# A two-layer decoder on one core: layer 0's attentions in a line of their own, one pair at a time

## The chip, the core and the metric

The kernel runs on one NeuronCore of a Trainium2 chip, in fp32 throughout. The metric is the device time of one execution in microseconds (us), lower is better. TensorE (PE) multiplies, VectorE (DVE), ScalarE (ACT) and GpSimd (POOL) do the rest, and SyncE (SP) issues all DMAs in one queue.

## The reference, cut to what matters

32 batches of 56 tokens with 128 features pass two decoder layers; each step is added to its input and normalized (post-norm).

```python
x = ln(x + self_attn(x))                      # layer 0: 16 heads of 8, window of 32 tokens
x = ln(x + cross_attn(q=x, k=ctx, v=ctx))     # one head, ctx is 32 x 1500 x 128
x = ln(x + moe_gelu(x))                       # 8 experts of 512 units, top 2
x = ln(x + recurrence(x))                     # layer 1: conv over 3 tokens, gated scan, gate
x = ln(x + tanh(g) * cross_attn16(x, ctx))    # 16 heads of 64 over the same 1500 rows
x = ln(x + moe_swiglu(x))                     # shared expert and 8 experts of 256, top 2
```

In both mixtures every expert is computed for every token, and the router's weight (zero outside the top 2) multiplies its output. Layer 1's cross-attention is the large piece: its key and value projections are folded into the queries and the output, so that per batch 16 x 56 = 896 query columns meet 1500 context rows directly.

## The kernel before, in words

Two batches make a pair (112 tokens, TP), and there are 16 pairs. Layer 0 and layer 1's recurrence work on groups (`GROUPS`): pair 0 alone, pair 1 alone, then two pairs at a time, seven times.

The program is written by a planner in Python. Each stage is a generator which emits some instructions and then yields a latency in us, the time that it wants to pass before its next step. A `Thread` wraps it and adds up the PE time that it has spent, by the kernel's own table of costs. The order in which the threads are stepped gives the order in which instructions are emitted; the framework's scheduler makes every engine's queue from it, and stays near to it. PE executes its queue in order, so an instruction whose input is late holds everything behind it.

- `attention()` is the main thread, layer 1's cross-attention. Each batch is two blocks of 512 and 384 query columns. A block has 12 score products (`s<-qo,amT`, each copied by ACT at L1007), their maximum (DVE L1010, L1018), a shift (L1092), an exponential (ACT L1095), and 12 value products per 128 columns (`v<-amN,s`). Scores of one block stand beside values of the block before.
- `pre(g)` is everything ahead of it for group g: `self_attention`, `cross_attention_0`, `experts_0`, `recurrent_mixer`, `queries_1`. One thread per group; the threads run one after the other. `since` and `part` give the share of `PRE_US` that is due at this point of the main thread.
- `post(k)` is everything behind it for pairs 2k and 2k+1: the output projection (`f<-qo,n`) and `experts_1`. The last two pairs take `experts_1` one by one.
- `opening()` takes pairs 0 and 1 before the main thread starts, the second of them in borrowed memory (`place["aside"]`).
- When the main thread comes to a pair whose group is not ready, `finish` steps that thread to its end with nothing of the main thread between.

All products of `pre` and `post` go through two PSUM banks (pool `p_f`, tag f); scores have three (s), values two (v), transposes one (t).

Names that matter below. `normalize` and `normalize_twice` are a chain: sum (DVE), `moments` (two DVE instructions), two POOL instructions (L353, L354), a scaling on DVE (L356); their results `y`, `h`, `py` are then transposed on PE (L156). In `self_attention`, scores go through DVE (L436, L443), POOL (L444) and ACT (L448) before PE transposes them (`f<-ident,big`). `top2` is some 20 small DVE instructions behind the router; `wmix` is its result. `experts_0` uses the Gelu table of ACT (L684), while Exp and Tanh are in another. `experts_1` loads gate, up and down weights of each routed expert (three DMAs of 128 KB, tile `w`), with three buffers:

```python
t = wst.tile([P, 3 * U1], F32, tag="w1", name="w1", bufs=3)
```

Its loop issues the load of expert e, then gate and up products of the expert before it, then the down product (`f<-w,h`) of the one before that. `load_x0` brings the context for `cross_attention_0` (`cxN`), which also writes the transposed context to DRAM (`memT`) for the main thread's `amT`.

Of the kernel before, what the change touches and what calls it, by code (L numbers as in the profile page):

```python
# [15 lines left out]
TP = 2 * S  # L16
# [47 lines left out]
PRE_US, POST_US, PAIR_US = 74.0, 31.0, 80.5  # L64
# [5 lines left out]
def decoder_kernel(  # L70
# [33 lines left out]
    place = {"aside": None}  # L104

    def bank(pool, tag):
        if pool is p_f and place["aside"]:
            pool, tag = p_s, "s"
        return pool.tile([P, 512], F32, tag=tag, name=tag)
# [34 lines left out]
    clock = {"pe": 0.0}  # L144

# [44 lines left out]
    qpad0 = const.tile([P, G, 64], F32, name="qpad")  # L190
# [118 lines left out]
    def wide_tile(tag, n=T, bufs=1):  # L309
        return work.tile([P, T], F32, tag=tag, name=tag, bufs=bufs)[:, :n]  # L310
# [27 lines left out]
    def to_features(tiles, tag):  # L338
        t = wide_tile(tag)[:, : len(tiles) * TP]
        nc.vector.tensor_copy(t, transposed(tiles))  # L340
        return t
# [31 lines left out]
    def ahead(a, b, tag="res", bufs=2):  # L373
        r = tok_tile(tag, bufs)
        nc.gpsimd.tensor_tensor(r, a, b, ALU.add)  # L375
        return r
# [9 lines left out]
    HOP, NORM, LOAD = 2.5, 6.0, 14.0  # L386


    def self_attention(xs):
        nj, nt = len(xs), len(xs) * TP  # L390
        xT = to_features(xs, "xT")
        res = [ahead(t, obias) for t in xs]
        yield HOP
        qT, kT, oT = wide_tile("qT0", nt), wide_tile("kT0", nt), wide_tile("oT0", nt)
        affine(qT, linear(sqw("wq0"), xT, nt), vcol("bq0"))
        yield 0
        affine(kT, linear(sqw("wk0"), xT, nt), vcol("bk0"))
        yield 0
        vs, kbs = [], []
        for j in range(nj):  # L400

            v = hidden_tile().rearrange("p u t -> p (u t)")[:TP, : H0 * 32]
            v = v.rearrange("p (h f) -> p h f", h=H0)
            nc.vector.tensor_tensor(
                v.rearrange("p (i r) f -> p i r f", i=4),
                linear(pair(xT, j), sqw("wv0"), D, TP)
                .rearrange("p (i f) -> p i f", i=4).unsqueeze(2).to_broadcast([TP, 4, 4, 32]),
                vmask[:TP].unsqueeze(1).to_broadcast([TP, 4, 4, 32]),
                ALU.mult,
            )  # L410
            kb = mid.tile([P, 4, TP], F32, tag="kb", name="kb", bufs=2)
            nc.gpsimd.tensor_tensor(
                kb,
                pair(kT, j).unsqueeze(1).to_broadcast([P, 4, TP]),
                hmask4.unsqueeze(2).to_broadcast([P, 4, TP]),
                ALU.mult,
            )
            vs.append(v)
            kbs.append(kb)
            yield HOP  # L420
        w = 4 * TP
        for j in range(nj):
            s = big_tile(0)[:TP]
            s3 = s.rearrange("p (h k) -> p h k", h=H0)
            mx = tiny.tile([TP, H0], F32, tag="mx16", name="mx16")
            for i0 in (0, 2):
                pss = []
                for i in (i0, i0 + 1):

                    r = slice(32 * i, 32 * i + 32)  # L430
                    ps = bank(p_f, "f")
                    mm(ps[:TP, :w], pair(qT, j)[r], kbs[j][r].rearrange("p h k -> p (h k)"))
                    pss.append(ps)
                for i, ps in zip((i0, i0 + 1), pss):
                    c = slice(4 * i, 4 * i + 4)
                    nc.vector.scalar_tensor_tensor(  # L436
                        s3[:, c, :],
                        ps[:TP, :w].rearrange("p (h k) -> p h k", h=4),
                        DH0**-0.5,
                        wmask.unsqueeze(1).to_broadcast([TP, 4, TP]),  # L440
                        ALU.mult, ALU.add,
                    )
                    nc.vector.tensor_reduce(mx[:, c], s3[:, c, :], AX.X, ALU.max)  # L443
                    nc.gpsimd.tensor_tensor(  # L444
                        s3[:, c, :], s3[:, c, :],
                        mx[:, c].unsqueeze(2).to_broadcast([TP, 4, TP]), ALU.subtract,
                    )
                    nc.scalar.activation(  # L448
                        s[:, i * w : (i + 1) * w], s[:, i * w : (i + 1) * w], AF.Exp
                    )  # L450
                yield 0
            yield 2.5
            st = big_tile(1)[:TP]
            st3 = st.rearrange("p (h q) -> p h q", h=H0)
            for i in range(4):
                ps = bank(p_f, "f")
                for h in range(4):
                    tr(ps[:TP, h * TP : (h + 1) * TP], s3[:, 4 * i + h, :])
                nc.scalar.copy(st[:, i * w : (i + 1) * w], ps[:TP, :w])
                yield 0  # L460
            yield HOP

            pz = bank(p_f, "f")
            for r in range(4):
                for i in range(4):
                    mm(
                        pz[32 * i : 32 * i + 32, :TP], vmask[:TP, r, :], st3[:, 4 * i + r, :],
                        start=(r == 0), stop=(r == 3),
                    )
            po = bank(p_f, "f")  # L470
            for r in range(4):
                for i in range(4):
                    mm(
                        po[32 * i : 32 * i + 32, :TP], vs[j][:, 4 * i + r, :],
                        st3[:, 4 * i + r, :], start=(r == 0), stop=(r == 3),
                    )
            rz = work.tile([P, TP], F32, tag="o0", name="o0", bufs=1)
            nc.vector.reciprocal(rz, pz[:, :TP])
            nc.vector.tensor_tensor(pair(oT, j), po[:, :TP], rz, ALU.mult)
            yield HOP  # L480
        ys = []
        for j in range(nj):
            ys.append(normalize(plus(linear(pair(oT, j), sqw("wo0"), D, TP), res[j]), "y"))
            yield 0
        yield NORM
        return ys


    def load_x0(pp):
        cxN = contexts_0()  # L490
        for i in range(2):
            b = 2 * pp + i
            load_context(cxN[i], b)

    def cross_attention_0(xs, g):
        nj, nt, nb = len(xs), len(xs) * TP, 2 * len(xs)
        cxN, qpad = contexts_0(), here(qpad0, "qpad")[:, :nb]
        xT = to_features(xs, "xT")
        res = [ahead(t, rowb("xbo0")) for t in xs]
        yield HOP  # L500
        qp, oT, vT = wide_tile("qT0", nt), wide_tile("oT0", nt), wide_tile("kT0", nt)
        affine(qp, linear(sqw("xq0"), xT, nt), vcol("xbq0"))
# [3 lines left out]
            linear(sqw("xk0"), qp, nt).rearrange("p (b s) -> p b s", b=nb),  # L506
# [3 lines left out]
        for p in range(nj):  # L510
            cxT = [big_tile(i) for i in range(2)]
            for i in range(2):
                for k in range(NS):
                    ps = bank(p_f, "f")
                    for c in range(CS):
                        tr(ps[:, c * PK : (c + 1) * PK], cxN[i][:, k * CS + c, :D])
                    copy = nc.vector.tensor_copy if k == 1 else nc.scalar.copy
                    copy(cxT[i][:, k * w : (k + 1) * w], ps[:, :w])
                    yield 0
                nc.sync.dma_start(memT[2 * GROUPS[g][p] + i], cxT[i][:, : CK * PK])  # L520
            yield 0.4


            pr = cxT[0]
            mx = tiny.tile([P, NS], F32, tag="mx", name="mx")
            for k in range(NS):
                ps = bank(p_f, "f")
                for i in range(2):
                    mm(
                        ps[64 * i : 64 * i + 64, :w], qpad[:, 2 * p + i, :],  # L530
                        cxT[i][:, k * w : (k + 1) * w],
                    )
                nc.scalar.copy(pr[:, k * w : (k + 1) * w], ps[:, :w])
                nc.vector.tensor_reduce(
                    mx[:, k : k + 1], pr[:, k * w : (k + 1) * w], AX.X, ALU.max
                )
                yield 0
            nm = tiny.tile([P, 1], F32, tag="nm", name="nm")
            nc.vector.tensor_reduce(nm, mx, AX.X, ALU.max, negate=True)
            for k in range(NS):  # L540
                nc.scalar.activation(
                    pr[:, k * w : (k + 1) * w], pr[:, k * w : (k + 1) * w], AF.Exp, bias=nm
                )
# [769 lines left out]
```

## Time and profile before

| | us |
|---|---|
| median of 3 runs | 2332.32 (2326.22 to 2332.54) |
| the profiled execution, its own time | 2330.03 |
| its span, first to last instruction | 2328.3 |
| PE busy in the span | 2214.2 (95%) |
| DVE, ACT, POOL busy | 1437.5, 1310.2, 251.8 |

The time is that of the launch as a whole; the span is some 2 us shorter. Busy time of PE counts overlapping products once. The mean granted PE clock is 0.984 of full speed. An entry such as `L147 PE MATMUL f<-xT,wu` names the line of the helper that emits all products (L147; L156 for transposes), so groups are told apart by tiles. One fp32 product is two MATMUL records.

### The profile page before, as it was taken

To read this page: it belongs to the slowest core of one execution; us is meant where nothing else is said; L and a number is where in the kernel's file an instruction comes from. 1 tells how busy PE (TensorE), PEld (TensorE's weight loads), DVE (VectorE), ACT (ScalarE), POOL (GpSimd) and SP (SyncE) were. 2 spreads that over 40 slices of the span, in tenths; PEclk is the share of its full clock that TensorE was granted. 3 is DMA by queue.
4 is the path that set the end of the run, shared out by engine and by line. 5 is a ranking of instruction groups with operands and counts; after the bars stand their busy time and mean duration, and the time that the engine had idled before them with its cause. 6 is when DMAs were issued, how large, how long until landed. Compare 5 with 4: busy or idle time off the path is not lost. (4 is left out here: it accounts for less than half of the span.)

```text
span 2328.3 us, 37425 instructions
## 1 busy us (share of the span) xinstructions
PE 2214.2 (95%) x14784; PEld 1736.3 (75%) x14784; DVE 1437.5 (62%) x2798; ACT 1310.2 (56%) x2279; POOL 251.8 (11%) x416
## 2 busy tenths in 40 slices
PE   7899998899999999999999999999999999999997
PEld 4766777577876788777887788768797778778787
DVE  4367554576366764676666665766656765566774
ACT  3455565556754667555655556564665555654652
POOL 3011001300023000210011100110001200100000
PEclk9899999999999999999999999999999999999999
DMA  6621322033311333114320153203331132211221
GB/s 185 178 74 29 107 54 86 16 81 91 97 48 30 80 104 105 29 36 126 92 76 17 54 134 91 65 14 81 107 111 32 28 107 71 68 27 41 69 83 37
DMA packets 164304, 172.21 MB, mean 74 GB/s; under 512 B 9465, under 2 KB 136865, under 8 KB 164001
## 3 DMA queue, kind: packets, MB, share of 16 engines
q1 hardware_dynamic: 164128, 169.82, 26.0%
q8 instruction: 117, 1.92, 0.3%
q14 instruction: 59, 0.48, 0.1%
HBM read 144.29 MB, written 25.49 MB: 73 GB/s over the span
## 5 line engine op out<-in xcount | busy, mean ns | idle before, releaser
L147 PE MATMUL v<-amN,s 125*128 125x129 f32 x5376 | 704.0, 277 | 6.1 <-ACT s L1095 3.6
L147 PEld LDWEIGHTS v<-amN,s 125*128 125x128 f32 x5376 | 665.4, 193 | 47.0 <-issue 25.6
L147 PE MATMUL s<-qo,amT 128*125 128x512 f32 (+1 forms) x1536 | 655.5, 547 | 3.4 <-ACT s L1007 3.1
L1007 ACT COPY s<-s 125x512 f32<-125x512 f32 (+1 forms) x768 | 396.8, 536 | 211.6 <-PE s L147 208.1
L1092 DVE TENSOR_TENSOR s<-s,nb 125x1536 f32<-125x1536 f32 (+1 forms) x256 | 395.4, 1556 | 61.8 <-ACT nb L1084 61.3
L1095 ACT ACTIVATE s<-s 125x1536 f32<-125x1536 f32 (+1 forms) x256 | 338.5, 1326 | 99.9 <-DVE s L1092 94.2
L147 PEld LDWEIGHTS s<-qo,amT 128*125 128x125 f32 x1536 | 264.7, 189 | 169.7 <-issue 94.5
L1010 DVE TENSOR_TENSOR m<-m,s 125x1024 f32<-125x1024 f32 (+1 forms) x256 | 280.8, 1097 | 79.4 <-ACT s L1007 75.5
L353 POOL TENSOR_SCALAR rs<-mv 112x1 f32<-112x1 f32 x126 | 44.2, 351 | 1562.9 <-DVE mv L347 1439.8
L1112 ACT ACTIVATE ao<-v,rz 128x128 f32<-128x128 f32 x224 | 80.5, 362 | 173.6 <-DVE rz L1110 170.4
L684 ACT ACTIVATE hT<-f,vec 128x224 f32<-128x224 f32 (+1 forms) x256 | 105.3, 435 | 100.9 <-PE f L147 98.4
L147 PE MATMUL f<-xT,wu 128*128 128x224 f32 (+1 forms) x512 | 135.6, 369 | 5.0 <-ACT hT L684 4.3
L147 PE MATMUL f<-wd,hT 128*112 128x128 f32 x960 | 126.2, 281 | 1.9 <-ACT hT L684 1.1
L147 PEld LDWEIGHTS f<-wd,hT 128*112 128x112 f32 x960 | 115.5, 181 | 15.4 <-ACT hT L684 3.9
L147 PE MATMUL f<-pxT,w 128*128 128x224 f32 (+1 forms) x576 | 119.4, 345 | 2.9 <-DMA w<-in_up_dram 1.1
L147 PEld LDWEIGHTS f<-pxT,w 128*128 128x128 f32 x576 | 98.7, 194 | 20.9 <-issue 4.4
L147 PEld LDWEIGHTS f<-xT,wu 128*128 128x128 f32 x512 | 86.7, 199 | 32.4 <-ACT hT L684 12.7
L1010 DVE TENSOR_TENSOR m<-s 125x1024 f32<-125x1024 f32 x64 | 69.6, 1087 | 54.3 <-ACT s L1007 54.2
L701 DVE SCALAR_TENSOR_TENSOR acc<-f,wmix,acc 112x128 f32<-112x128 f32 x120 | 41.6, 348 | 86.4 <-PE f L147 86.0
L444 POOL TENSOR_TENSOR big<-big,mx 112x448 f32<-112x448 f32 x60 | 75.5, 1276 | 146.4 <-PE f L147 71.0
L1084 ACT COPY nb<-t 125x512 f32<-125x512 f32 x64 | 34.0, 531 | 94.2 <-PE t L156 93.7
L156 PE MATMUL f<-ident,big 112*112 112x112 f32 (+1 forms) x420 | 62.8, 282 | 22.2 <-ACT big L448 15.6
(282 smaller groups left out, 2619.6 us busy)
## 6 DMA issues: line engine op xcount, KB each, us to landing
amT<-memT SPq DMA_DIRECT2D x32, 750.0 KB
amN<-in_mem_dram SPq DMA_DIRECT2D x34, 672.0 KB
memT<-big SPq DMA_DIRECT2D x30, 750.0 KB
cxN<-in_mem_dram SPq DMA_DIRECT2D x30, 672.0 KB
wu<-in_wup_dram SPq DMA_DIRECT2D x72, 256.0 KB
wd<-in_wdn_dram SPq DMA_DIRECT2D x72, 256.0 KB
w<-in_gate_dram SPq DMA_DIRECT2D x72, 128.0 KB
w<-in_up_dram SPq DMA_DIRECT2D x72, 128.0 KB
```

What stands on the lines that cost most here:

```text
L147: nc.tensor.matmul(ps, lhsT=lhsT, rhs=rhs, start=start, stop=stop)
L156: nc.tensor.transpose(ps, in_, ident[:k, :k])
L353: nc.gpsimd.tensor_scalar(rs, mv[:, 1:2], mul, add, ALU.mult, ALU.add)
L444: nc.gpsimd.tensor_tensor(s3[:, c, :], s3[:, c, :], mx[:, c].unsqueeze(2).to_broadcast([TP, 4, TP]), ALU.subtract,)
L684: nc.scalar.activation(hT[:, u, :], linear(ws[0][:, u * D : (u + 1) * D], xT, nt), AF.Gelu, bias=vec[:, C_BUP + e * nu + u : C_BUP + e * n ...
L701: nc.vector.scalar_tensor_tensor(acc[j], down(last[1], last[0][1], nu, j), w[:, j, e - 1 : e], acc[j], ALU.mult, ALU.add,)
L1007: nc.scalar.copy(s[:, c, :], ps[:PK, :n])
L1010: nc.vector.tensor_tensor(m, a, s[:, c - 1 : c + 1, :], ALU.max)
L1084: nc.scalar.copy(nb, ps[:PK, :n])
L1092: nc.vector.tensor_tensor(c, c, nb.unsqueeze(1).to_broadcast([PK, 3, n]), ALU.add)
L1095: nc.scalar.activation(c, c, AF.Exp)
L1112: nc.scalar.activation(o, po[:, :D], AF.Copy, scale=rz)
```

## The change

The attentions of layer 0 are taken out of the group threads. `front(pp)` does self- and cross-attention of one pair; `back(g)` waits until the fronts of its pairs are there and does experts, recurrence and queries of the group. Fronts form one line (`front_line`), backs another (`back_line`), and both are stepped beside the main thread and the posts, each by a plan of where it should begin and end, counted in pairs of the main thread.

```diff
-PRE_US, POST_US, PAIR_US = 74.0, 31.0, 80.5
+FRONT_US, BACK_US, POST_US, PAIR_US = 18.5, 37.0, 31.0, 81.5
+BANK_US = 1.3
...
-    def self_attention(xs):
-        nj, nt = len(xs), len(xs) * TP
-        xT = to_features(xs, "xT")
+    def self_attention(x):
+        xT = to_features([x], "xT")
...
-    def cross_attention_0(xs, g):
+    def cross_attention_0(x, pp):
...
+    def front(pp):
+        t = xin.pop(pp)
+        if 1 < pp < NPAIR - 1:
+            xin[pp + 1] = load_x(pp + 1)
+        t = yield from self_attention(t)
+        fronts[pp] = yield from cross_attention_0(t, pp)
...
+    def back(g):
+        if g > 1:
+            for pp in GROUPS[g]:
+                while pp not in fronts:
+                    yield None
+            expert[g] = yield from experts_0([fronts.pop(pp) for pp in GROUPS[g]])
+            yield NORM
+        yield from behind_experts(expert.pop(g), g)
...
+    front_end = {pp: pp - 3.1 for pp in range(1, NPAIR)}
+    front_end.update({1: 0.0, 2: 0.45, 3: 0.9, 4: 1.4, 5: 2.1})
+    front_line = [
+        (Thread(front(pp)), front_end[pp - 1], front_end[pp]) for pp in range(2, NPAIR)
+    ]
+    back_line = [(backs[0], 0.0, 0.6)] + [
+        (backs[g - 1], front_end[GROUPS[g][-1]], GROUPS[g][0] - 0.3) for g in range(2, NG)
+    ]
...
-        g = next((g for g in range(1, NG) if not pres[g].over), None)
-        if g == 1:
-            until(pres[1], 1e9)
-        elif g is not None:
-            since = 0 if g == 2 else GROUPS[g - 1][0]
-            part = (at - since) / (GROUPS[g][0] - since)
-            until(pres[g], PRE_US * part / 0.88)
+        along(front_line, FRONT_US, at)
+        along(back_line, BACK_US, at)
```

A thread is now stepped only when the f banks have had some rest: `taken` holds the PE time at which banks of this pool were last taken, and a step that takes two banks (it follows a `Two` yield) waits for the last of them.

```diff
+    class Two(float):
+        pass
...
+        def ready(self, late):
+            held = taken[-1 if self.two else -2] + (0 if late else BANK_US)
+            return not self.over and clock["pe"] >= max(self.at, held)
...
     def until(th, us):
-        while not th.over and th.at <= clock["pe"] and th.spent < us:
+        while th.spent < us and th.ready(th.spent < us - 5.0):
```

Fronts and backs no longer share tiles (`xb`, `ub`, `gb`, `xq`, `small`, `yb`, `ya` are new names beside `xT`, `kT0`, `qT0`, `oT0`, `big0`, `y`), and some tiles have one buffer less. Among these is the routed weight of `experts_1`. The last pair's routed weights are loaded together into the score tile that the last block leaves free, and its products rotate over seven banks instead of two.

```diff
-            t = wst.tile([P, 3 * U1], F32, tag="w1", name="w1", bufs=3)
+            if kept is not None:
+                return kept[e]
+            t = wst.tile([P, 3 * U1], F32, tag="w1", name="w1", bufs=2)
...
-                yield 1.2
+                yield 2.4
...
+    def load_last_weights():
+        t = sbig.tile([P, CK, 512], F32, tag="s512", name="s512").rearrange("p c n -> p (c n)")
+        for e in range(E):
+            last_weights.append(t[:, e * 3 * U1 : (e + 1) * 3 * U1])
...
+            if pp == NPAIR - 1:
+                place["free"] = ((p_f, "f"), (p_s, "s"), (p_v, "v"), (p_f, "f"), (p_s, "s"))
...
                 old = (prev, os)
+                if prev[:2] == (B - 1, 0):
+                    load_last_weights()
```

The arithmetic is the same. Counted in the two programs, PE has 70 products of 112 columns (128x112) where it had 35 of 224 (128x224); ACT has 1139 activations instead of 1104 and 125 table loads instead of 95; DVE has 14 copies more; the number of DMAs (594) is the same.

## The prediction, made before the changed kernel ran

> **What bounds the kernel now.** I read the page first, then the busy time by stage, then who waits for whom, then the timeline at the places that these name. On the page, PE is the engine of the bound, and its row of tenths and its clock row tell where it is not full:
>
> ```profile
> PE 2214.2 (95%) x14784; PEld 1736.3 (75%) x14784; DVE 1437.5 (62%) x2798; ACT 1310.2 (56%) x2279; POOL 251.8 (11%) x416
> ...
> PE   7899998899999999999999999999999999999997
> ...
> PEclk9899999999999999999999999999999999999999
> ```
>
> So at most 114 us of idle PE time (2328.3 - 2214.2) and what the clock takes can be won by a new order. By stage (us of the stage, busy us of PE, PEld, DVE, ACT, POOL, clock, DMA share, GB/s):
>
> ```profile
> 0.00:150.00 150.00, 126.13 (x828) 91.52 (x829) 64.85 (x179) 62.98 (x148) 24.98 (x68) 0.93 0.58 164
> 150.00:300.00 150.00, 143.99 (x1021) 106.99 (x1021) 103.36 (x156) 92.27 (x154) 19.56 (x24) 1.00 0.21 58
> 300.00:480.00 180.00, 156.01 (x1026) 120.28 (x1027) 95.42 (x198) 99.76 (x168) 34.03 (x42) 0.93 0.18 51
> 480.00:2290.00 1810.00, 1761.64 (x11743) 1394.69 (x11743) 1157.91 (x2206) 1051.04 (x1800) 171.72 (x278) 0.99 0.25 71
> 2290.00:2329.00 39.00, 26.41 (x172) 22.84 (x171) 15.93 (x61) 4.16 (x12) 1.48 (x4) 0.87 0.17 53
> ```
>
> The opening idles for 24 us, the stretch where group 1's rest and group 2 are rushed (300 to 480) for 24, the long steady part for 48, the tail for 12. Who makes PE wait, in us, times and longest:
>
> ```profile
> PE f L156 <- DVE h L356: 19.7, 17, 2.6
> PE f L156 <- ACT big L448: 15.6, 14, 4.7
> PE t L156 <- DVE rz L1110: 6.9, 5, 2.7
> PE f L156 <- ACT big L459: 5.9, 8, 1.5
> PE f L156 <- DVE wmix L627: 3.1, 2, 2.8
> PE f L156 <- DVE y L356: 1.9, 2, 1.7
> PE f L147 <- DVE oT L770: 1.6, 1, 1.6
> PE f L147 <- DVE xT L728: 1.4, 1, 1.4
> ```
>
> All but the third are layer 0's and the recurrence's own chains: PE reaches a transpose before DVE, POOL and ACT have made its input. Those seven are 49.2 us. Two places of the timeline, and the reload of a routed weight in the tail:
>
> ```profile
> 400.39 0.45 PE L156 MATMUL f<-ident,h 112*128 112x112 f32 x1 [2.47 <-DVE h L356]
> 440.71 1.89 PE L156 MATMUL f<-ident,big 112*112 112x112 f32 x8 [4.74 <-ACT big L448]
> ...
> 2315.28 0.33 SPq L825 DMA_DIRECT2D w<-in_gate_dram  x1
> 2315.65 0.44 SPq L825 DMA_DIRECT2D w<-in_up_dram  x1
> 2319.54 0.67 PE L147 MATMUL f<-pxT,w 128*128 128x112 f32 x4 [1.13 <-DMA w<-in_up_dram]
> ```
>
> **The change, part by part.** My measure is the distance: the PE work between the product that starts a chain and the instruction that needs its end, taken from PE's order in the two programs, each instruction at its usual step in this trace (a value product 0.23 us, score products 0.86 and 0.65, other products 0.22 at 112 columns and 0.38 at 224, a transpose 0.1). A chain that takes longer than its distance makes PE wait for the difference.
>
> *Chains of fronts and backs.* From 300 us on, before has the transposes of h at distances of 0.1 to 5.3 us (the close ones; others have 8 and more) and waits of 0.9 to 2.6 at 3 to 4: the chain takes 5 to 6. The changed order has 5.0 to 13.5 there. From the score products of self-attention to the transposes of their exponentials, before has 2.2 to 4.9; the changed order has 5.0 to 9.7 from pair 7 on; of the earlier ones only pair 5 has less (2.9 to 4.2). The router's wmix goes from 5.5 to 6.6 to 7.3 to 11.0. Of the 49.2 us, some 5 lie in the opening, whose code hardly changes; 44 are in reach. In the rush around 440, POOL's L444 took 8.00 us for two instructions (1.28 each is its mean): such a chain is longer than the new distances too. I take 40. Also better: an f bank is taken again within 1 us of PE work after its last product 255 times, before 361. I give nothing for it.
>
> *Clock.* The records grant 0.93 in 300 to 480: 0.07 x 180 = 12.6 us lost; 0.99 in the steady part, some 10 more. The Trainium skill ("TensorE: Matmul & The Clock Gate", section "Why this matters for your kernels") asks only that no idle gap exceed some 3 us, which would put all the loss in that stretch on the one wait of 4.74, less than 2 us by its window of 3.4 us at half rate. The trace has seven waits of 1 to 3 us there and loses 12.6, so short gaps in a row cost clock here: with the gaps goes most of it. I take 9; the rule would give 2.
>
> *Tail.* From 2302.4 to 2323.5 an expert takes some 2.65 us, since gate products need the two f banks that th and h still hold; one reload costs 1.13 more. With seven banks, DVE's work sets it: nine times th 0.39, h 0.39, pacc 0.35 is 10.2, and some 20 small ones of top2 at 0.16 are 3.5: near 14 us instead of 21 or 22. I take 8. The 24 loads into the score tile are released some 14 us of PE work before the first is needed; issues of 0.33 to 0.43 us make 10 us for all, and each is needed 1.4 us after the one before. Hidden; without that cover, the tail would give back 3.
>
> *Products.* 70 at 0.235 (`f<-qo,n`, 60.3 us for 256 products) against 35 at 0.42 to 0.44: +1 to +2. PE's order changes its stream 205 times more often; a change costs 15 ns over the usual step (1787 of them between 480 and 2290): +3. Together +5.
>
> *ACT.* 56 more activations of 112 columns at 0.353 and 14 of 0.263, less 28 at 0.447 and 7 at 0.351: +8.5 us. Table loads go from 95 to 125, as Gelu is spread between Exp and Tanh. The row of one:
>
> ```profile
> L684 ACT ACT_TABLE_LOAD x47 | 60.3, 1283 | 1.3 <-PE f L147 0.5
> ```
>
> 30 x 1.283 = 38.5 us. The Trainium skill ("ScalarE: Activation LUTs", section "What ACT_TABLE_LOAD costs") speaks against the change more strongly: 1283 ns and a drain of some 1380, 2.66 for a switch, or 80 us. Here the next instruction starts 20 ns after the load (333.99 + 1.28, then 335.29), so the trace's 38.5 stands. ACT comes to 1357 us, 59%. It touches PE where a score bank is not copied in time (`PE s L147 <- ACT s L1007`: 3.1 us now). Bounds 0 (three s banks hide it) and 38.5 (none hidden); a tenth is near to what the 95 loads do today: +4. By the rule it would be +8.
>
> *Reload of routed weights with two buffers.* This is the new wait. With three, the load of expert e waited for a down product long done; with two it waits for the down product of e-2, which stands just before the need. In the changed order 34 of the 64 reloads have 2.3 to 3.3 us of PE work from that release to the first gate product; the up product comes 0.4 to 0.8 later. From issue to the last semaphore update, a gate load takes 2.3 us (median), an up load 2.5, issued 0.37 later; a quarter of the up loads take over 3.4, when a context load (5.2 to 9.9) shares the DMA engines, at most 7.3. So alone it fits within 0.2 us. In each group the first of the short ones follows a cxN load by 2 us: about 3 us late, and the next about 0.5. Five groups at 3.3 make 16, the rest some 1: I say 15. Bounds: 0 (in before, five reloads at 2.7 to 4.7 caused no wait) and 65 (below). Behind a waiting reload on SP stand wu, wd, xin and the second half of cxN; they have 16 us and more before their need, and amT keeps 11 or more in steady running: nothing for those. cxN itself is released 46 us and more ahead, before 16.
>
> *What is late next:* the maxima's transposes (`t<-ident,m`, waits on L1110 and L1018, 10 us), untouched.
>
> The sum: -40 - 9 - 8 + 5 + 4 + 15 = -33. The profiled execution took 2330.03, 2.3 below the median, so 2297 by its own clock and 2299 against the median.
>
> **The rivals.**
>
> 1. *Reloads are late everywhere (slower).* In the interleaved order the DMA engines are seldom free at the moment of a reload. At a landing of 5.0 us, midway between the quarter's 3.4 and the 7.3, up weights are there 5.5 us after the release, needed after 3.6: 1.9 x 34 = 65 in place of 15. The sum is +17: 2349. It decides from (33 + 15) / 34 = 1.4 us per reload on. For it: `w<-in_up_dram` on the chain of the tail, 3.75 us. Against: the five of before.
> 2. *The chains grow with the interleaving (no change).* DVE, ACT and POOL serve two more streams in turn, POOL's 8.00 us shows how far it can go, and only a third of gaps and clock is won: -13 - 3 - 8 + 24 = 0: 2332. Against it: distances grew by more than the waits were.
> 3. *Reloads and tables are hidden (better).* -57 + 5 = -52: 2280.
>
> **How the numbers follow.** A run of this kernel can be told from no change at about 0.3%, 7 us. Forecast 0.55, rival 1 0.13, rival 2 0.12, rival 3 0.20. Faster by over 0.3%: nearly all of the forecast, rival 3 and a third of rival 2: 0.77; within: 0.10; slower: 0.13. The range leaves out rival 1 and the slow part of rival 2: 2270 to 2328.
>
> **What would show it.** Right: `DVE h L356` and `ACT big L448` under 8 us together in PE's waits; clock 0.97 or more between 300 and 480; the tail's experts at 1.5 us; 125 table loads. A new row `PE f L147 <- DMA w` of some 15 us is my term; 50 or more is rival 1. Wrong: PE's idle time is as long as before under other names, or `s<-qo,amT` waits for ACT by 15 us or more.

## The result, and the profile after

The changed kernel takes 2347.19 us (median of 5, 2339.44 to 2352.06) against 2332.32: 1.0071 times the time before, 95% interval 1.0042 to 1.0099. It is slower by 15 us, where 33 us less were forecast. The profiled execution took 2352.06, its span is 2350.4. On the page, the busy time, the tenths and the clock of PE:

```profile
PE 2227.4 (95%) x14854; PEld 1753.8 (75%) x14854; DVE 1438.4 (61%) x2812; ACT 1359.2 (58%) x2344; POOL 251.5 (11%) x416
...
PE   7889999999999999989999899998999999999998
...
PEclk9799999999999999999999999999999999999999
```

PE's row has fewer deep holes at the start (the rush of group 2) and new ones in the middle. By stage, in the same stretches of time as before, though the work in them has shifted (columns as before; the last stretch begins at 2290 too and so holds more than the tail):

```profile
300.00:480.00 180.00, 167.55 (x1122) 132.12 (x1122) 104.17 (x207) 110.58 (x188) 29.38 (x43) 0.94 0.25 64
480.00:2290.00 1810.00, 1743.16 (x11518) 1379.04 (x11518) 1137.05 (x2183) 1081.86 (x1826) 172.75 (x276) 0.98 0.24 68
2290.00:2351.00 61.00, 49.86 (x385) 45.71 (x383) 32.14 (x95) 15.35 (x33) 2.22 (x6) 0.93 0.27 79
```

The rush idles 12 us instead of 24: won as forecast. The steady part idles 67 us (1810 - 1743.16) instead of 48, and its clock is 0.98 instead of 0.99. PE's waits, in us, times and longest:

```profile
PE v L155 <- ACT s L1100: 12.8, 7, 3.0
PE f L155 <- DMA w<-in_gate_dram: 11.1, 10, 2.6
PE t L164 <- ACT ao L1117: 9.7, 5, 2.4
PE f L164 <- DVE pacc L880: 9.1, 5, 2.1
PE f L164 <- ACT hT L677: 6.7, 4, 2.2
PE t L164 <- DVE nm L1076: 6.0, 6, 1.5
PE f L164 <- ACT big L452: 5.4, 5, 1.8
...
PE f L164 <- DVE h L364: 1.8, 2, 1.4
```

The chains that the change was to shorten are gone: h fell from 19.7 to 1.8, big from 15.6 to 5.4. In their place stand waits that were short before: for the exponential of the main thread (3.6 before), for its copy `ao` (2.6 in two rows), for a routed weight (1.1), for `pacc` (1.1). The rows of before:

```profile
PE v L147 <- ACT s L1095: 3.6, 3, 1.6
...
PE v L147 <- ACT ao L1112: 2.3, 3, 0.9
...
PE f L147 <- DMA w<-in_up_dram: 1.1, 1, 1.1
PE f L147 <- DVE pacc L886: 1.1, 3, 0.4
...
PE t L156 <- ACT ao L1112: 0.3, 1, 0.3
```

Three of the first five rows after the change are ACT being late. Its table loads:

```profile
L677 ACT ACT_TABLE_LOAD x62 | 79.5, 1283 | 2.2 <-PE f L155 1.1
...
L452 ACT ACT_TABLE_LOAD x14 | 18.0, 1283 | 0.2
```

L677 is Gelu (L684 before, 47 loads), L452 the exponential of self-attention, which had a single load of its own before (L448): a back's Gelu now stands between two exponentials of a front. One such place, from ACT's and PE's rows of the timeline:

```profile
1045.20 0.58 ACT L452 ACTIVATE big<-big 112x448 f32<-112x448 f32 x1 [2.59 <-POOL big L448]
...
1046.08 0.47 PE L164 MATMUL t<-ident,ao 128*128 128x128 f32 x1 [1.83 <-ACT ao L1117]
...
1047.51 1.28 ACT L677 ACT_TABLE_LOAD   x1
...
1049.27 1.28 ACT L452 ACT_TABLE_LOAD   x1
...
1051.62 1.28 ACT L677 ACT_TABLE_LOAD   x1
...
1053.51 0.57 PE L164 MATMUL f<-ident,big 112*112 112x112 f32 x4 [1.47 <-ACT hT L677]
1053.75 1.28 ACT L1100 ACT_TABLE_LOAD   x1
...
1055.05 1.48 ACT L1100 ACTIVATE s<-s 125x1536 f32<-125x1536 f32 x1
...
1056.58 1.23 PE L155 MATMUL v<-amN,s 125*128 125x129 f32 x4 [1.85 <-ACT s L1100]
```

ACT first waits 2.59 us for POOL with the main thread's copy `ao` queued behind, and PE waits 1.83 for that copy. Then four loads in 7.5 us; the main thread's exponential comes 9 us after the one before it (1045.93), and PE waits again. The other new wait, with PE's rows and SP's (SPq):

```profile
1141.61 0.60 PE L155 MATMUL f<-w,h 128*112 128x128 f32 x4
1142.25 0.33 SPq L819 DMA_DIRECT2D w<-in_gate_dram  x1
...
1147.37 0.81 PE L155 MATMUL f<-pxT,w 128*128 128x224 f32 x3 [2.22 <-DMA w<-in_gate_dram]
```

The reload is issued when the down product (`f<-w,h`) is over, behind a part of `cxN` (issued at 1140.33), and its weights are there 5.1 us later. Four waits of this kind, each on a reload issued 1.9 us after a part of `cxN`, hold 8.4 of the 11.5 us.

**A ledger.** For the experiments I split each profiled span into three: the waits ahead of PE instructions, summed; the time lost in half-speed windows (length times missing share of the clock); and the rest, PE's work at full clock. Waits, clock and rest are those of one profiled execution, the median is that of all.

| kernel | median us | ratio to before, 95% interval | waits | clock | rest | table loads |
|---|---|---|---|---|---|---|
| before | 2332.32 | | 109 | 38 | 2181 | 95 |
| after | 2347.19 | 1.0071 (1.0042 to 1.0099) | 118 | 58 | 2175 | 125 |
| e1 after, Tanh | 2288.49 | 0.9806 (0.9791 to 0.9821) | 85 | 32 | 2173 | 1 |
| e2 before, Tanh | 2304.66 | 0.9873 (0.9857 to 0.9890) | 91 | 27 | 2183 | 1 |
| e3 after, split | 2325.05 | 0.9964 (0.9952 to 0.9976) | 106 | 43 | 2174 | 125 |
| e4 after, serial | 2366.71 | 1.0144 (1.0130 to 1.0158) | 126 | 47 | 2195 | 65 |
| e5 split, Tanh | 2269.55 | 0.9737 (0.9717 to 0.9758) | 78 | 20 | 2170 | 1 |
| e6 split, gated | 2298.46 | 0.9863 (0.9842 to 0.9884) | 86 | 32 | 2179 | 95 |
| e7 before, tail | 2324.65 | 0.9971 (0.9958 to 0.9985) | 109 | 32 | 2179 | 95 |
| e8 split, f3 | 2318.80 | 0.9947 (0.9926 to 0.9968) | 100 | 47 | 2170 | 121 |
| e9 loads, value | 2289.89 | 0.9813 (0.9800 to 0.9827) | 79 | 32 | 2177 | 129 |
| e10 loads, score | 2277.48 | 0.9763 (0.9747 to 0.9778) | 76 | 27 | 2177 | 129 |
| e11 before, gated | 2324.55 | 0.9958 (0.9943 to 0.9973) | 106 | 32 | 2179 | 73 |
| e12 before, w2 | 2375.74 | 1.0185 (1.0161 to 1.0208) | 140 | 70 | 2176 | 91 |
| e13 loads, burst | 2369.44 | 1.0147 (1.0128 to 1.0166) | 123 | 60 | 2183 | 129 |
| e14 gated, short shift | 2309.80 | 0.9884 (0.9863 to 0.9904) | 87 | 40 | 2182 | 103 |
| e15 gated, f3 | 2298.93 | 0.9846 (0.9824 to 0.9869) | 91 | 49 | 2163 | 91 |
| e16 burst elsewhere | 2351.42 | 1.0073 (1.0057 to 1.0089) | 121 | 52 | 2182 | 129 |

Beside the experiments the kernel before took 2330.9 to 2335.8 (medians), so a difference between experiments of different rounds is good to some 5 us. In these two profiles the change made PE's own work shorter (-6) and lost 9 in waits and 19 in clock, together 22 us where the medians are 15 apart: the profiled execution was the slowest of the five. Clock moves between executions of one kernel. By the granted clock of every run the loss is 37 us before and 52 after, +15; so, too, 42 for e3, 19 for e5 and 56 for e12, whose profile also is of its slowest run.

### The profile page after: what moved, and what is told of

The parts are those of the page before. It is cut to its first block, busy times and chain, and to the rows that moved or that the text cites. A ratio compares the mean times of both kernels' runs of the same rounds, so it can differ in the third digit from the quotient of the medians.

```text
span 2350.4 us, 37566 instructions
## 1 busy us (share of the span) xinstructions
PE 2227.4 (95%) x14854; PEld 1753.8 (75%) x14854; DVE 1438.4 (61%) x2812; ACT 1359.2 (58%) x2344; POOL 251.5 (11%) x416
## 5 line engine op out<-in xcount | busy, mean ns | idle before, releaser
L155 PE MATMUL v<-amN,s 125*128 125x129 f32 x5376 | 720.8, 279 | 12.8 <-ACT s L1100 12.8
L155 PEld LDWEIGHTS v<-amN,s 125*128 125x128 f32 x5376 | 681.1, 194 | 53.1 <-issue 30.3
L677 ACT ACTIVATE hT<-f,vec 128x224 f32<-128x224 f32 (+1 forms) x256 | 107.7, 437 | 86.7 <-PE f L155 84.7
L155 PE MATMUL f<-xb,wu 128*128 128x224 f32 (+1 forms) x512 | 142.4, 376 | 8.9 <-DMA wu<-in_wup_dram 4.2
L155 PE MATMUL f<-wd,hT 128*112 128x128 f32 x960 | 131.0, 284 | 1.1 <-DVE acc L694 0.5
L155 PE MATMUL f<-pxT,w 128*128 128x224 f32 (+1 forms) x512 | 107.0, 349 | 12.1 <-DMA w<-in_gate_dram 11.1
L155 PEld LDWEIGHTS f<-xb,wu 128*128 128x128 f32 x512 | 87.0, 203 | 38.7 <-issue 14.3
L155 PEld LDWEIGHTS f<-pxT,w 128*128 128x128 f32 x512 | 88.8, 190 | 22.5 <-issue 13.9
L164 PEld LDWEIGHTS f<-ident,big 112*112 112x112 f32 (+1 forms) x420 | 51.5, 165 | 48.2 <-issue 20.6
L1115 DVE RECIPROCAL rz<-v 128x1 f32<-128x1 f32 x224 | 35.9, 160 | 78.1 <-PE v L155 77.6
```

Source lines behind the costliest of these rows:

```text
L155: nc.tensor.matmul(ps, lhsT=lhsT, rhs=rhs, start=start, stop=stop)
L164: nc.tensor.transpose(ps, in_, ident[:k, :k])
L677: nc.scalar.activation(hT[:, u, :], linear(ws[0][:, u * D : (u + 1) * D], xT, nt), AF.Gelu, bias=vec[:, C_BUP + e * nu + u : C_BUP + e * n ...
L1115: nc.vector.reciprocal(rz, po[:, D : D + 1])
```

## The experiments

Three theories: A, ACT is late (table loads, and work queued behind its waits); R, the routed weights' reloads; O, the order itself (streams and banks in turn).

### e1 and e2: no table loads

```diff
-  linear(ws[0][:, u * D : (u + 1) * D], xT, nt), AF.Gelu,
+  linear(ws[0][:, u * D : (u + 1) * D], xT, nt), AF.Tanh,
```

e1, on the changed kernel:

> The changed kernel with Tanh in place of Gelu in layer 0's experts (the function computed changes, the work does not), so that Exp and Tanh share one table and the 125 table loads (160 us of ACT) fall to a few. Theory A (ACT is late: table loads and head-of-line waits on ACT put the new stalls on PE): the waits for ACT s L1100, ao L1117 and hT L677 (29 us together) and most of the extra clock loss (19 us) go: about 2347 - 25 - 12 = 2310, and this kernel becomes faster than the unchanged kernel with the same replacement. Theory R (routed weights with two buffers): only the little that ACT cost before goes: 2340, still 12 to 20 above the unchanged kernel with Tanh. Theory O (the order itself: PE turns between streams, f banks are taken again too early): 2335 to 2342, same sign against the unchanged one.

e2, on the kernel before:

> The unchanged kernel with Tanh in place of Gelu in layer 0's experts (the function computed changes, the work does not); 95 table loads (122 us of ACT) fall to a few. Theory A: its chains wait for DVE and POOL rather than for table loads, so only some 5 to 8 us: 2325. Theories R and O: the same, 2325.

Measured 2288.49 and 2304.66. An activation takes 437 and 436 ns instead of 437 and 435, so the work is the same without the loads. The framework's scheduler also gave some of it another place: of ACT's activations and copies about a tenth stand elsewhere in its queue (2007 of 2219 keep their order in e1), and what that does is part of the difference. With the loads go 59 us in the changed kernel and 29 in the old one, more than any theory gave. Without them the changed order is 16 us the faster one. Of e1's waits:

```profile
PE v L155 <- ACT s L1100: 3.9, 1, 3.9
...
PE t L164 <- ACT ao L1117: 2.4, 1, 2.4
```

The two rows fell from 22.5 to 6.3. Where the old kernel pays is seen from the stages: at the start of the main thread's pair 4 (counted from 0), e2 is 26.4 us ahead of before (669.6 against 696.0), and at the end of the span 26.6. In these two profiles its loads cost up to that point, and the 56 behind it nothing. The changed one pays 17.4 up to there (711.2 against 728.6) and 42.8 for the 88 loads after: its pairs 4, 6, 8 and 10 take 147 to 149 us, in e1 137 to 139.

### e3: the reloads

```diff
-  t = wst.tile([P, 3 * U1], F32, tag="w1", name="w1", bufs=2)
-  for i, w in enumerate((gate1, up1, down1)):
-      nc.sync.dma_start(t[:, i * U1 : (i + 1) * U1], w[:, e * U1 : (e + 1) * U1])
+  for w, tag in ((gate1, "w1g"), (up1, "w1u"), (down1, "w1d")):
+      t = wst.tile([P, U1], F32, tag=tag, name=tag, bufs=2)
+      nc.sync.dma_start(t, w[:, e * U1 : (e + 1) * U1])
```

> The changed kernel with each routed weight in three tiles (gate, up, down), two buffers each, in the same memory: gate and up of expert e+1 no longer wait for the down product of e-1, only the down part does, and that is needed much later. Theory R: the waits for w (11.5 us) go and the low-clock windows that they start go too: 2347 - 11 - 8 = 2328. Theory A and O: the waits for w go, but PE then waits for ACT and banks at the next instruction instead; 2340 to 2344.

Measured 2325.05, 22 us less: R's number and more, and already faster than the kernel before. No wait for a routed weight is left among PE's. The 22 come from waits and clock: 12 and 14 in the ledger's two profiles, 12 and 10 with the clock of all runs. Both e1 and e3 are large, so A and R both hold, and neither is the whole.

### e4: fronts and backs one after the other

```diff
-  front_end = {pp: pp - 3.1 for pp in range(1, NPAIR)}
...
+  for g in range(2, NG):
+      t0 = 0.3 if g == 2 else GROUPS[g - 1][0]
+      d = (GROUPS[g][0] - 0.25 - t0) / (2 * FRONT_US + BACK_US)
+      for pp in GROUPS[g]:
+          front_line.append((Thread(front(pp)), t0, t0 + FRONT_US * d))
+          t0 += FRONT_US * d
+      back_line.append((backs[g - 1], t0, t0 + BACK_US * d))
```

> The changed kernel with its plan set so that fronts and backs do not stand beside each other: within the pairs that a group has, the two fronts come first, one after the other, and then the back (as in the unchanged kernel); all code of the change otherwise stays, two buffers for w and the new tail included. Theories A and O: the new stalls (s L1100, ao L1117, hT L677, pacc) go, the old chains (DVE h, ACT big, some 35 us) come back; with the tail's -6 and the reloads' +11 about 2335. Theory R: no change from 2347 or worse, since the reloads stay short.

Measured 2366.71: slower than the changed kernel by 20 where 12 less were expected. The old chain is back (`DVE h` 29.4 us of waits), and PE waits 19.8 for score copies as well. Loads are only 65. But waits in all are just 8 us more and the clock's loss is less; the ledger has 20 us more in the rest, over many groups of products, and what makes it is open. The pairs of this plan are uneven (127 to 131 and 154 to 159 us in turn), so it is not a clean measure of the interleaving: theory O, that the order harms by itself, is not settled by e4 but by e5.

### e5: both costs away

It joins the edits of e1 and e3.

> e3 and e1 together: routed weights in three tiles, and Tanh in place of Gelu in layer 0's experts (the function computed changes, the work does not). What is left of the change is its order, its products and its tail. If the two costs add up (reloads 22 us, tables 59 us): 2347 - 22 - 59 = 2266, 38 us under the unchanged kernel with Tanh, which is what the prediction's terms for order, clock, tail and products allow (-52) less some. If both act through the same waits of PE: 2278 to 2288, no better than e1.

Measured 2269.55: the two add up (2266 was the sum). This is what the order, the products and the tail are worth by themselves: 35.1 us against e2 (32 by the ratios). So the order side by side is a gain, and theory O falls.

### e6 and e11: a plan that knows the tables

The core of e6's edit, on e3; `phase["exp"]` is true while the main thread has exponentials pending:

```diff
+  if held_off and self.table is Gelu and phase["exp"]:
+      return False
...
-  while th.spent < us and th.ready(th.spent < us - 5.0):
+  ahead = 16.0 if th.table is Gelu else 0.0
+  while th.spent < us + ahead and th.ready(th.spent < us - 5.0, th.spent > us - 20.0):
```

> e3 (three tiles), and a plan that knows the tables: the back's Gelu steps are taken while the main thread is in score products and has no exponential pending, up to 16 us of PE work ahead of its plan, and the exponentials of self-attention are held while the back stands before a Gelu. 95 table loads instead of 125, all else computed as in the reference. If a table load costs the 0.5 us that it costs on average in the changed order (59 / 125): 2325 - 15 = 2310; if the last 30 cost 1.0 each (59 - 29 over 30): 2295. If only the order matters, not the loads: 2325 or worse, since the steps come in bunches.

e11 has the same for Gelu on the kernel before with the new tail:

> The unchanged kernel with the new tail (e7) and the same table-aware plan as e6 in its own group threads: 73 table loads instead of 95. By 0.30 us a load (28.9 / 95): 2325 - 7 = 2318; by 0.9 a load: 2305. The order of the change is worth having only if this stays above e6's 2298: theory A and the sum of e5 against e2 (-35 in all, -29 without the tail) say 2318 against 2298. If the gain of e6 was the bunching of Gelu alone, this one reaches 2298 too.

e6 took 2298.46: 27 us less than e3 (24 by the ratios), or 0.8 to 0.9 us for each load that went, and 1.4% faster than the kernel before. The wait for the main thread's exponential is 4.9 us instead of e3's 11.6, and the largest row left is

```profile
PE f L164 <- DVE pacc L888: 9.4, 4, 2.3
```

e11 took 2324.55, as e7 without the plan: 22 loads less gained nothing clear of the noise. They went from where the old order hid them: the 21 of the first 480 us stayed. So a load has no fixed price, and the new order is needed for e6's time.

### e7: the tail alone

```diff
+  if prev[:2] == (B - 1, 0):
+      load_last_weights()
...
-  for y in (yield from experts_1(xs)):
+  if pp == NPAIR - 1:
+      place["free"] = ((p_f, "f"), (p_s, "s"), (p_v, "v"), (p_f, "f"), (p_s, "s"))
+  for y in (yield from experts_1(xs, last_weights if pp == NPAIR - 1 else None)):
```

> The unchanged kernel with the new tail alone: the last pair's routed weights all in the score tile, its products over the seven banks in turn. By the changed kernel's tail (29.3 us against 35.5) 2333 - 6 = 2327; the prediction's term was -8: 2325. If the loads that now run together delay the last blocks: 2333 or more.

Measured 2324.65, 6.2 us less than before beside it (2330.87). The stretch after the last value product is 29.2 us instead of 35.5, as in the changed kernel (29.3).

### e9, e10, e13, e16: the same 128 loads, put elsewhere

All on e5. One column of Gelu forces a load, and the next Exp another.

```diff
+  if k == 1:                                # e9: second exponential of each block
+      nc.scalar.activation(spot[:PK], c[:, 0, 0:1], AF.Gelu)
...
+  if c in (5, 7):                           # e10: behind two score copies
+      nc.scalar.activation(spot[:PK], s[:, c, 0:1], AF.Gelu if c == 5 else AF.Exp)
...
+  burst = b % 2 == 0 and q0 == 0            # e13: all four of 16 blocks (e16: b % 2 == 1)
+  if burst:
+      nc.scalar.activation(spot[:PK], c[:, 0, 0:1], AF.Gelu)
```

> e5 (three tiles, Tanh for Gelu, no table changes) with one column of Gelu set in front of the second exponential of every block: it forces two table loads there, 128 in all, 164 us of ACT, beside the value products. Nothing else changes (the extra result is not used). Theory A with the mean price of the changed order (0.44 us a load): 2270 + 57 = 2327. With the price of the last 30 loads (0.9): 2385. If loads are hidden wherever they stand and the cost in the changed kernel came from the crowding of ACT with three streams' work: 2270 to 2280.

> e5 with the same 128 table loads set in the middle of the score products: one column of Gelu behind the copy of the sixth score bank, one column of Exp behind the eighth. Theory A: three s banks give ACT about 2 us there, a load takes 1.28 and the copies 0.54 against 0.86 of PE, so ACT catches up: 2270 to 2285, well under e9. If a load costs the same anywhere: as e9.

> e5 with 128 table loads as in e9, but in bursts: one column of Gelu in front of all four exponentials of the first block of every second batch (16 blocks, eight loads each within some 15 us), none elsewhere. Crowding theory: eight loads are 10.3 us of ACT within 15 us, where ACT is already 0.6 busy; each burst puts 2 to 4 us of waits on PE and a half-speed window: 16 x 4 = 64 on e5, about 2330, or 44 and more above e5. If the price is per load and not per place: as e9, 2290.

> e13 with its 16 bursts moved to the first block of the other batch of each pair, where neither self-attention's exponentials nor the experts' activations stand beside them (there are three exponentials of cross-attention and the tanh of the recurrence). If a burst of eight costs by itself: as e13, +100 on e5, 2370. If it needs the third stream's own work on ACT in the same place: nearer to e9, +20 to +45, 2290 to 2315.

Against e5's 2269.55: +8 beside score copies (the intervals of the two ratios overlap), +20 beside exponentials, +100 and +82 in bursts. The same number of loads costs 0.06, 0.16, 0.78 and 0.64 us each. PE's wait for the exponential in e9, then in e13:

```profile
PE v L155 <- ACT s L1104: 6.5, 5, 2.0
```
```profile
PE v L155 <- ACT s L1105: 37.4, 26, 1.9
```

Inside a burst of e16:

```profile
839.71 1.28 ACT L1104 ACT_TABLE_LOAD   x1
841.59 1.28 ACT L1105 ACT_TABLE_LOAD   x1
...
844.42 0.94 PE L155 MATMUL v<-amN,s 125*128 125x129 f32 x6 [1.89 <-ACT s L1105]
```

A part of the exponentials (a quarter of a block) now comes every 5 us from ACT (starts at 837.84 and 842.88). PE, which waited for the part before at 839.38, has 3.1 us of work until it needs this one (844.42 - 839.38 - 1.89), so it waits again at each further part. One pair of loads in a block (e9) is caught up before the next: e9's waits are 1 us above e5's, and the ledger has its 20 us in clock (12) and in the rest (7), which this reading doesn't explain. The bursts cost without self-attention beside them too; beside it 18 us more. The old order had eleven loads between 853 and 885 with waits of at most 0.15 us: its exponentials also came 5.2 us apart there (866.84, 871.99, 877.25), but PE had the experts' products to do between them. That this work is what hid them was not tried by itself.

### e12: two buffers in the old order

```diff
-  t = wst.tile([P, 3 * U1], F32, tag="w1", name="w1", bufs=3)
+  t = wst.tile([P, 3 * U1], F32, tag="w1", name="w1", bufs=2)
```

> The unchanged kernel with two buffers for the routed weights instead of three, nothing else. If the reloads cost what they cost because the new order puts the need close behind the release: within 3 us of 2332. If two buffers cost 22 us in any order: 2354.

Measured 2375.74, 43 us more. The new row, and one of six places in the tail:

```profile
PE f L147 <- DMA w<-in_gate_dram: 35.6, 18, 3.3
```
```profile
2353.86 2.02 PE L147 MATMUL f<-pxT,w 128*128 128x112 f32 x8 [2.47 <-DMA w<-in_gate_dram]
```

This kernel still has the old tail, where experts follow each other with nothing between, and there each of the last six waits some 2.45 us for its gate weight: 14.7 of the 35.6 us. The stretch after the last value product takes 55.7 us instead of 35.5. The changed kernel has no reloads in its tail. Ahead of the tail that leaves some 23 us (43 less 20) for two buffers in the old order, about the 22 of the new one. So the second expectation holds once the tail is set apart: the loss is that of two buffers, and the new order does not cause it. Whether spreading the experts out (`yield 2.4` for 1.2) softens it isn't shown.

### e8, e14, e15: what holds pacc

e8 is e3 with three f banks and two s banks, e15 the same on e6; e14 is e6 with the shift ahead of an exponential in three pieces:

```diff
-  p_s = ctx.enter_context(tc.tile_pool(name="p_s", bufs=3, space=PSUM))
+  p_s = ctx.enter_context(tc.tile_pool(name="p_s", bufs=2, space=PSUM))
...
-  p_f = ctx.enter_context(tc.tile_pool(name="p_f", bufs=2, space=PSUM))
+  p_f = ctx.enter_context(tc.tile_pool(name="p_f", bufs=3, space=PSUM))
...
-  nc.vector.tensor_tensor(c, c, nb.unsqueeze(1).to_broadcast([PK, 3, n]), ALU.add)
+  for i in range(3):
+      nc.vector.tensor_tensor(c[:, i, :], c[:, i, :], nb, ALU.add)
```

> e3 with three f banks and two s banks in place of two and three. Theory O (f banks are taken again too early: the waits for DVE pacc, ACT hT and DVE acc, some 25 us in e3, are waits for a bank): these go, 2325 - 15 = 2310. Theory A: what PE waits for is ACT, and with two s banks it also waits for the copies of scores (L1010): 2325 to 2345.

> e6 with the shift in front of each exponential (DVE, 125x1536, 1.74 us) issued as three instructions of 125x512: shorter pieces for what queues behind it on DVE, 512 more instructions. If DVE's queue holds pacc, xT and pr (18 us of waits with e6's others): 8 to 12 us less with the clock, 2288. If the pieces only cost: 512 x 0.06 us of DVE, 103 table loads instead of 95: 2300 to 2310.

> e6 with three f banks and two s banks (e8's change on e6), 91 table loads. If the number of banks holds those waits: 2298 - 6 = 2292, as e8 against e3. With two s banks PE waits for score copies (8.7 us in e6 with three): 2300 to 2315.

e8 took 2318.80, and its interval overlaps e3's; e15 2298.93, no different from e6; e14 2309.80, 11 us above e6, though the intervals overlap. The wait for `pacc` is 9.0 us with three banks on e3 (e8), 10.7 with short pieces (e14) and 9.4 in e6; but with three banks on e6 (e15) it is 0.6. So the length of the piece ahead of it is not its cause, and on the number of banks the two tries differ: that stays open. In e6's timeline DVE has a scaling that waited 1.05 us for POOL, a shift of 1.75 and a maximum of 0.67 ahead of `pacc` in its queue; which of them would have to move stays open. The other expected gains were given up to score copies: 11.4 us of waits for L1011 in e8, and for L1019 18.6 in e14 and 20.4 in e15 against e6's 8.7; in e15 a new wait of 15.6 us for `xq`, which ACT copies, stands beside them.

## Why the prediction was wrong

Three terms of the sum were mis-sized, in us (the measured ones are differences of medians, and make up the result of +14 to +15):

| term | forecast | measured | from |
|---|---|---|---|
| order: chains, clock, tail, products | -52 | -35 | e5 - e2 |
| table loads and ACT | +4 | +27 | (e3 - e5) - (before - e2) |
| reload of routed weights | +15 | +22 | after - e3 |

By the ratios, or with the two costs taken away in the other order, the tables measure 23 to 32, the reloads 16 to 25 and the order -32 to -35.

- **ACT was the step with the largest miss**, 23 us; alone it would have left -10, and the other two made the rest. "A tenth is near to what the 95 loads do today" was not read from anything: today's 95 cost 29 us (e2). And 30 more loads were priced like the 95, by their number. What counted was their place: both orders have up to eight loads within 20 us, but in the new one they stand where the main thread's exponential and copy are needed, and two more streams' work is on ACT. The text had 125 loads and 1357 us of ACT right, and that said little: ACT is 58% busy, and late where it matters.
- **What is late next.** "Untouched" was said of the maxima's transposes alone. From e2 to e5 waits fell by 13 us (91 to 78) where 40 was forecast for the chains and part of 8 for the tail; clock fell by 7 and the rest by 13. The chains named went, and `pacc`, `xT` and `pr` of DVE came (9.1, 4.3 and 4.0 us in e5). Their cause is open, and so is that of the shorter rest, for which the products' term had +5.
- **Reloads.** The waits were sized well: 11.5 us against 15, behind a `cxN` load as said. Five late ones of about 3 us behind `cxN` were forecast, and four of 1.8 to 2.6 us came. What was missed is their clock, 10 to 14 us. The lower bound of 0 rested on five short reloads of before that caused no wait; with two buffers in that same order they do (e12).
- **Clock.** Forecast -9, measured +15 (37 to 52 over all runs). Every wait term needs its clock beside it: e3 against e5 has 28 us of waits and, over all runs, 22 of clock. The remark that short gaps in a row cost clock was used for the gain only, not for the new waits.
- **Right:** h and big together 7.2 us (under 8 was named), the rush's idle time halved (its clock stayed at 0.94, not 0.97), the tail's experts near 1.6 us, 6 us saved of 8, 125 table loads. The products' +5 is not seen: the rest fell by 6 from before to after.

Of the rivals, the first is refuted in size (reloads at 65 us, measured 22): that its 2349 lies beside the measured 2347 is luck. The third is refuted as well. The second, that DVE, ACT and POOL serve two more streams, named the right engine among others; but the chains that it let grow became shorter, and the lateness fell on the main thread's exponential and copy, which had no price in it. "PE's idle time is as long as before under other names" was the sign named for a wrong forecast, and it is what the profile shows (waits of 118 us for 109).

## What to carry to other kernels

Price an in-order engine by place, not by its share: between two results that PE needs, add up what stands in its queue (loads of tables, waits for other engines) and compare it with PE's work in between. When streams are put side by side, a table switch that was hidden in one can fall between the other's; let the plan hold one table's work until the other's is over. With two buffers, release each part of a tile by its own last use, as e3's three tiles do, before a third buffer is bought; and give each short wait of PE its clock too, here about 0.8 us for each us (e3 against e5, after against e3).

## What was not expected of the hardware

- The Trainium skill ("TensorE: Matmul & The Clock Gate", section "Why this matters for your kernels") sets some 3 us as the idle gap to stay under. Here shorter ones lower the clock: of the 25 waits of 1.4 to 2.5 us of the changed kernel between 480 and 2240, 15 have a window at half speed beside them (from the wait's start to 3.5 us after its end); of the 13 from 0.5 to 1.4, two.
- What decides in these traces is the sum of idle time, not the single gap. In all 18 kernels the granted clock changes on a grid of 3.41 us. Between 480 and 2240, a full-speed window of that grid in which PE idled 2.0 us or more in total was followed by a half-speed window in 70 of 70 cases; with 1.4 to 2.0 us in 47 of 124; with less than 1.4 in 11 of 8930. In 10 of the 70 no single gap made the 2.0 us, so waits that are harmless alone add up. A wait of 2 us and more that fell across the edge of two windows, with less than 2.0 in either, was followed by half speed in 8 of 32 cases. So the place on the grid decides too. A half-speed window costs up to 1.7 us of clock.
- 128 table loads, 164 us of ACT, cost 8 us where they stand beside score copies (e10), and 100 in bursts of eight (e13).
